# Splitting the PSUM banks of an attention's scores by the engine that empties them, on one Trainium2 core

## The chip, the core and the metric

The program runs on one core of one Trainium2 chip. The metric is the device time of one execution in microseconds, the median over the runs shown. A core has TensorE (matmuls, transposes and the loads of their weights), VectorE, ScalarE, GpSimd, the queues that start transfers, and a PSUM of eight banks of 128 partitions x 512 fp32 values, into which TensorE writes. In the profile the engines are PE (PEld for weight loads), DVE, ACT, POOL and SP.

## The reference

A block on x of 1024 rows and 512 columns, all in fp32, batch 1. Four layers with residuals stand one after the other:

```python
x = x + attn_a(layernorm(x))      # 32 heads of width 16, rotary, causal, full softmax
x = x + ffn(layernorm(x))         # 8 experts of rank 16, top 2, beside a dense base
x = x + attn_b(layernorm(x))      # 32 query heads, 8 key heads of width 128, alibi
x = x + ffn(layernorm(x))
```

The change touches the first attention alone. Cut to what matters:

```python
xq, xk, xv = (x @ w.T).reshape(B, T, 32, 16)       # for wq, wk, wv
xq, xk = rotary_pos_emb(xq), rotary_pos_emb(xk)
scores = einsum('bqhd,bkhd->bhqk', xq, xk) * 16 ** -0.5
probs = softmax(where(causal, scores, -1e30))
out = einsum('bhqk,bkhd->bqhd', probs, xv).reshape(B, T, 512) @ wo.T
```

## The kernel before

The first attention takes about the first 413 us of the span. Heads are padded from 16 to 32 values, so that four heads fill the 128 partitions: there are eight groups of four heads (`NCA` = 8, index c; the head inside a group is j).

The scores are made twice. **Row scores** (`row_scores`, L296; tiles named s) have queries on partitions; VectorE reduces each tile to the negated maximum of every row (`maxima`, L311: a TENSOR_REDUCE at L319 for unmasked pieces, a custom masked reduce at L322 for the others). The maxima are transposed (`with_maxima`, L333, tile tp_m), copied, and put by four small transfers into a spare row of qT, so that **column scores** (`col_scores`, L347; tiles named sT, keys on partitions) come out with the maximum already subtracted. A bf16 matmul of an identity and a mask is added on the diagonal (L372), and ScalarE takes the exponential of each tile (`exponentials`, L374) into p. `product` (L376) multiplies the values by p, in pieces of four matmuls of 32 output columns each.

A score matmul contracts 32 rows, those of one head, so the matmuls of four heads use four row groups of TensorE and can run side by side. Each is made of two fp32 passes.

`step(rc, cc, n)` (L433) does step n (0 to 9) for the row scores of group rc and the column scores of group cc. In the main loop (L477) rc = c + 1 and cc = c, and a step has two halves. A half makes two column tiles and two row tiles, in turn: sT, s, sT, s (`drain` takes one matmul from each generator in turn). The heads are crossed: with rows of heads 0 and 1 go columns of heads 2 and 3, and the other way round. After each half stand VectorE's maxima and ScalarE's exponentials, and then one piece of a product that is three steps old, as long as there is one left (L460, L461). In the seven passes c = 0 to 6 both kinds are made; in the last pass only column scores, and before the main loop the row scores of group 0 are made alone, four tiles at a time (L468 to L474), between the projections.

The projections (`project_a`, L150) take each block of 128 rows through layernorm, a transpose to channels (L206), the projections pj_q, pj_k and pj_v (L176), the rotation by ScalarE and VectorE (L182), and the transposes back into qT and kT (`to_rows`, L192): per block tp_aq and tp_ak, each in two halves. The half with c0 = 0 is copied by VectorE, the other by ScalarE.

Every one of these tiles takes one whole bank. All but the product's accumulator come out of one pool of seven banks, tag "s":

```python
ps_s = ctx.enter_context(tc.tile_pool(name="a_s", bufs=7, space=PSUM))
ps_o = ctx.enter_context(tc.tile_pool(name="a_o", bufs=1, space=PSUM))
```

A pool hands out the bank that is planned to come free first, and TensorE's first matmul into a tile waits until the last reader of the bank's former tile has ended. Each engine takes its instructions in the order of the program that is built; a few of them are placed by the planner and not by the source.

After the last pass `tail` (L996) gathers and projects the first two blocks of the output (tp_ao, pm_ao) around the last normalization (tp_o, L403 to L419), and the feed-forward layer takes over.

Of the kernel before, what the change touches and what calls it, by code (L numbers as in the profile page):

```python
# [9 lines left out]
F32 = mybir.dt.float32  # L10
# [4 lines left out]
PSUM = bass.MemoryType.PSUM  # L15

P = 128
T = 1024
NT = T // P
C = 512  # L20
KC = C // P
QC = 512
# [42 lines left out]
class Block:  # L65
# [58 lines left out]
    def attention_a(self, ctx_pool, wqT, wkT, wvT, rot, midway, tail):  # L124

        nc, tc = self.nc, self.tc

        xnT = ctx_pool.tile([P, NT, KC, P], F32, tag="o", name="xnTa")
        xnTs = [xnT[:, i] for i in range(NT)]
        with ExitStack() as ctx:
            ap = ctx.enter_context(tc.tile_pool(name="a_qkv", bufs=1))
            qT = ap.tile([P, NCA, T], F32, tag="qT", name="qT")
            kT = ap.tile([P, NCA, T], F32, tag="kT", name="kT")
            v_p = ap.tile([P, NT, HA + 1, DA + 1], F32, tag="v_p", name="v_p")  # L140
            nc.gpsimd.memset(v_p[:, :, :HA, DA : DA + 1], 1.0)
            nc.gpsimd.memset(v_p[:, :, HA, :], 0.0)
            ps_s = ctx.enter_context(tc.tile_pool(name="a_s", bufs=7, space=PSUM))
            ps_o = ctx.enter_context(tc.tile_pool(name="a_o", bufs=1, space=PSUM))
            pt = ctx.enter_context(tc.tile_pool(name="a_pt", bufs=5))
            work = ctx.enter_context(tc.tile_pool(name="a_x", bufs=4))
            project_qk, project_v = self.project_a(ap, pt, work, ps_s, xnTs, qT, kT, v_p, wqT, wkT, wvT, rot)
            return self.attend_a(ctx_pool, pt, work, ps_s, ps_o, qT, kT, v_p, project_qk, project_v, midway, tail)

    def project_a(self, ap, pt, work, ps_s, xnTs, qT, kT, v_p, wqT, wkT, wvT, rot):  # L150

        nc = self.nc

        w = {}

        def load(n, src, queue):
            w[n] = pt.tile([P, KC, C], F32, tag="p", name=f"w{n}")
            queue.dma_start(w[n], src.rearrange("(k p) n -> p k n", p=P))

        load("q", wqT, nc.scalar)  # L160
        rt = ap.tile([P, 4, NT], F32, tag="rot", name="rot_sb")
        nc.sync.dma_start(rt, rot)
        load("k", wkT, nc.sync)
        for i in range(2, NT):
            self.load_x(i)
        load("v", wvT, nc.sync)
        for n in range(6):
            self.transpose4(ps_s, [self.ident] * 4, f"i{n}", tag="s")
        rows = {}
        for n, fill in (("q", 0.0), ("k", 1.0)):  # L170
            t = pt.tile([P, 2, HA, PADA], F32, tag="p", name=f"r{n}")
            nc.gpsimd.memset(t[:, :, :, DA : DA + 1], fill)
            nc.gpsimd.memset(t[:, :, :, DA + 1 : PADA], 0.0)
            rows[n] = [t[:, a] for a in range(2)]

        def project(i, n):  # L176
            ps = ps_s.tile([P, C], F32, tag="s", name=f"pj_{n}{i}")
            for kc in range(KC):
                nc.tensor.matmul(ps, lhsT=xnTs[i][:, kc, :], rhs=w[n][:, kc, :], start=(kc == 0), stop=(kc == KC - 1))  # L179
            return ps  # L180

        def rotate(i, n, r, ps):  # L182
            cos, sin = rt[:, r, i : i + 1], rt[:, r + 1, i : i + 1]
            xs = work.tile([P, C], F32, tag="w", name=f"xs_{n}{i}")
            nc.scalar.activation(xs, ps, AF.Copy, scale=sin)
            pv = ps.rearrange("p (h d two) -> p h d two", d=DA // 2, two=2)
            sv = xs.rearrange("p (h d two) -> p h d two", d=DA // 2, two=2)
            dv = rows[n][i % 2][:, :, :DA].rearrange("p h (d two) -> p h d two", two=2)
            nc.vector.scalar_tensor_tensor(dv[:, :, :, 0], pv[:, :, :, 0], cos, sv[:, :, :, 1], ALU.mult, ALU.subtract)
            nc.vector.scalar_tensor_tensor(dv[:, :, :, 1], pv[:, :, :, 1], cos, sv[:, :, :, 0], ALU.mult, ALU.add)  # L190

        def to_rows(i, n, dst):  # L192

            for c0 in range(0, NCA, 4):
                src = [rows[n][i % 2][:, (c0 + c) * 4 : (c0 + c + 1) * 4, :].rearrange("p h d -> p (h d)") for c in range(4)]
                ps = self.transpose4(ps_s, src, f"a{n}{i}_{c0}", tag="s")
                copy = nc.scalar.copy if c0 else nc.vector.tensor_copy
                copy(dst[:, c0 : c0 + 4, i * P : (i + 1) * P], ps)

        pending = []  # L200

        def project_qk():
            def layernorm(i):
                return self.normalized(i, work.tile([P, C], F32, tag="w", name=f"xn_a{i}"), "a", in_order=True)

            def columns(i, xn):  # L206
                self.channels(xn, xnTs[i], ps_s, f"a{i}", tag="s")

            columns(0, layernorm(0))
            for i in range(NT):  # L210
                ps = project(i, "q")
                xn = layernorm(i + 1) if i + 1 < NT else None
                rotate(i, "q", 2, ps)
                if i + 1 < NT:
                    columns(i + 1, xn)
                rotate(i, "k", 0, project(i, "k"))
                while pending:
                    to_rows(*pending.pop(0))
                pending.extend([(i, "q", qT), (i, "k", kT)])
                yield  # L220

        def project_v():
            for i in range(NT):
                ps = project(i, "v")
                while pending:
                    to_rows(*pending.pop(0))
                nc.scalar.copy(v_p[:, i, :HA, :DA], ps.rearrange("p (h d) -> p h d", d=DA))
                yield

        return project_qk(), project_v()  # L230

    def attend_a(self, ctx_pool, pt, work, ps_s, ps_o, qT, kT, v_p, project_qk, project_v, midway, tail):
        nc, tc = self.nc, self.tc
        HC = P // PADA
        with ExitStack() as ctx:
            cp = ctx.enter_context(tc.tile_pool(name="a_c", bufs=1))
            qk = ctx.enter_context(tc.tile_pool(name="a_qk", bufs=2))
            o_sb = []

# [47 lines left out]
            def row_pieces(n):  # L287
                return list(placed(by_rows[n], lambda i, kc: min(QC, (i + 1) * P - kc * QC)))
# [7 lines left out]
            def row_scores(c, n, heads, made):  # L296

                for j in heads:
                    made[j] = ps_s.tile([P, QC], F32, tag="s", name=f"s{c}_{n}_{j}")
                for i, kc, at, end in row_pieces(n):  # L300
                    for j in heads:
                        nc.tensor.matmul(  # L302
                            made[j][:, at:end],
                            lhsT=qT[rows_of(j), c, i * P : (i + 1) * P],
                            rhs=kT[rows_of(j), c, kc * QC : kc * QC + end - at],
                            start=True,
                            stop=True,
                        )
                        yield
# [23 lines left out]
            def with_maxima(c, half):  # L333

                rows = HC * NT // 2
                ps = ps_s.tile([P, QC], F32, tag="s", name=f"tp_m{c}{half}")[:rows, :P]
                nc.tensor.transpose(ps, neg(c, half).rearrange("p h i -> p (h i)"), self.ident)
                t = qk.tile([P, P], F32, tag="negT", name=f"negT{c}_{half}")[:rows, :]
                nc.scalar.copy(t, ps)
                for j in range(HC):  # L340
                    row = j * PADA + DA
                    nc.sync.dma_start(
                        qT[row : row + 1, c, half * QC : (half + 1) * QC].rearrange("o (i t) -> o i t", t=P),
                        t[j * NT // 2 : (j + 1) * NT // 2, :],
                    )

            def col_scores(c, n, heads, made):  # L347

                pieces = col_pieces(n)
                for j in heads:  # L350
                    made[j] = ps_s.tile([P, QC], F32, tag="s", name=f"sT{c}_{n}_{j}")
                for x, (qc, b, at, end) in enumerate(pieces):
                    for j in heads:
                        nc.tensor.matmul(  # L354
# [48 lines left out]
            def normalize(c, qc, oT):  # L403
                if not o_sb:
                    o = ctx_pool.tile([P, NT, C], F32, tag="o", name="o")
                    o_sb.extend(o[:, i] for i in range(NT))
                ps = self.transpose4(ps_s, [oT[:, i * P : (i + 1) * P] for i in range(4)], f"o{c}{qc}", tag="s")
                pv = ps.rearrange("p a (h d) -> p a h d", d=PADA)
                os = qk.tile([P, 4, HC, DA + 1], F32, tag="os", name=f"os{c}_{qc}")
                nc.scalar.copy(os, pv[:, :, :, : DA + 1])  # L410
# [698 lines left out]
```

## Time and profile before

| what | value |
|---|---|
| median of 3 runs | 1683.34 us (1683.14 to 1686.43) |
| the profiled execution: its time | 1683.11 us |
| its span, first to last instruction | 1681.3 us |
| instructions | 32166 |
| granted TensorE clock | 1.000 |
| first attention's main loop, seven passes | 122 to 386 us |

The profile is of one execution. A row of the timeline gives start, length, engine, line, operation, output and inputs, shapes and count, and in brackets how long the engine idled before it and what ended that. Names in it leave out numbers: s stands for every row-score tile, sT for every column-score tile. An engine counts as busy as soon as one of its instructions runs, so four matmuls side by side and one alone look the same in the share of busy time.

### The profile page before, as it was taken

To read this page: it belongs to the slowest core of one execution; us is meant where nothing else is said; L and a number is where in the kernel's file an instruction comes from. 1 tells how busy PE (TensorE), PEld (TensorE's weight loads), DVE (VectorE), ACT (ScalarE), POOL (GpSimd) and SP (SyncE) were. 2 spreads that over 40 slices of the span, in tenths; PEclk is the share of its full clock that TensorE was granted. 3 is DMA by queue.
4 is the path that set the end of the run, shared out by engine and by line. 5 is a ranking of instruction groups with operands and counts; after the bars stand their busy time and mean duration, and the time that the engine had idled before them with its cause. 6 is when DMAs were issued, how large, how long until landed. Compare 5 with 4: busy or idle time off the path is not lost.

```text
span 1681.3 us, 32166 instructions
## 1 busy us (share of the span) xinstructions
PE 1652.6 (98%) x13016; PEld 940.7 (56%) x13016; DVE 1103.0 (66%) x2856; ACT 542.1 (32%) x1217; POOL 347.8 (21%) x508
## 2 busy tenths in 40 slices
PE   9999999999999999999999999999999999999988
PEld 5544444344555667556655665756655665566654
DVE  3556666662653886776677667676677766776773
ACT  2315555555111332233233223223223322322220
POOL 2000000000312332222123212222222321221140
PEclk9999999999999999999999999999999999999999
DMA  5000000001003201100200200110020020000001
GB/s 195 1 1 2 2 2 2 2 2 38 2 24 88 65 2 41 49 26 26 64 26 26 61 30 1 51 38 26 26 64 26 26 71 26 1 27 27 2 1 50
DMA packets 60868, 52.06 MB, mean 31 GB/s; under 512 B 5744, under 2 KB 47472, under 8 KB 60720
## 3 DMA queue, kind: packets, MB, share of 16 engines
q1 hardware_dynamic: 59408, 46.06, 9.2%
q0 software_dynamic: 784, 2.90, 0.4%
q8 instruction: 102, 1.67, 0.4%
q10 hardware_dynamic: 528, 1.05, 0.2%
q14 instruction: 46, 0.38, 0.1%
HBM read 30.98 MB, written 2.10 MB: 20 GB/s over the span
## 4 chain that ended last, share of the span: by engine, by line
PE 87%; DVE 10%; ACT 1%; POOL 1%; issue 1%; DVEq 0%; ACTq 0%; POOLq 0%
PE o L835 13%; PE pq L745 12%; PE s L791 12%; PE wo L642 9%; PE sT L354 7%; PE kv L700 7%; PE oT L389 5%; PE s L302 4%; PE pm_f L599 3%; PE or L835 3%; DVE p L793 3%; DVE nm L797 2%; DVE pT L818 2%; PE pj_v L179 2%; PE pm_ao L993 2%; PE pj_k L179 2%
## 5 line engine op out<-in xcount | busy, mean ns | idle before, releaser
L803 POOL TENSOR_SCALAR p<-p,rs 128x128 f32<-128x128 f32 (+7 forms) x256 | 190.8, 747 | 750.6 <-DVE rs L802 685.7
L800 ACT ACTIVATE p<-p,nm 128x128 f32<-128x128 f32 (+7 forms) x256 | 198.1, 774 | 453.4 <-DVE nm L798 443.0
L793 DVE SCALAR_TENSOR_TENSOR p<-s,rq,rel 128x512 f32<-128x512 f32 (+3 forms) x384 | 227.1, 605 | 119.4 <-PE s L791 118.8
L791 PE MATMUL s<-kT,qT 128*128 128x512 f32 (+3 forms) x768 | 294.8, 492 | 1.8 <-DVE p L793 1.5
L745 PE MATMUL pq<-xnTb,wq 128*128 128x512 f32 x512 | 246.2, 599 | 0.0
L642 PE MATMUL wo<-wo,oT 128*128 128x512 f32 x512 | 241.8, 594 | 3.4 <-DVE x L647 1.9
L791 PEld LDWEIGHTS s<-kT,qT 128*128 128x128 f32 x768 | 141.2, 190 | 165.8 <-issue 126.1
L835 PEld LDWEIGHTS o<-pT,va 32*128 32x128 f32 x5632 | 215.7, 185 | 28.5 <-DVE rs L802 11.8
L835 PE MATMUL o<-pT,va 32*128 32x128 f32 (+7 forms) x5632 | 224.6, 313 | 0.8
L818 DVE STREAM_TRANSPOSE pT<-p 128x640 f32<-128x640 f32 (+4 forms) x256 | 172.1, 673 | 73.1 <-PE o L835 54.7
L374 ACT ACTIVATE p<-sT 128x512 f32<-128x512 f32 (+1 forms) x320 | 157.5, 555 | 113.4 <-PE sT L372 70.9
L797 DVE TENSOR_REDUCE nm<-p 128x1 f32<-128x128 f32 (+7 forms) x256 | 188.2, 736 | 3.6
L302 PE MATMUL s<-kT,qT 32*128 32x512 f32 (+3 forms) x768 | 181.9, 522 | 0.0
L354 PE MATMUL sT<-qT,kT 32*128 32x512 f32 (+3 forms) x768 | 155.7, 521 | 0.0
L642 PEld LDWEIGHTS wo<-wo,oT 128*128 128x128 f32 x512 | 93.8, 190 | 87.5 <-issue 72.4
L745 PEld LDWEIGHTS pq<-xnTb,wq 128*128 128x128 f32 x512 | 92.3, 190 | 87.9 <-issue 80.2
L700 PE MATMUL kv<-wkv,xnTb 128*128 128x256 f32 x512 | 116.7, 382 | 4.4 <-DVE nm L798 4.0
L700 PEld LDWEIGHTS kv<-wkv,xnTb 128*128 128x128 f32 x512 | 95.8, 190 | 26.2 <-DVE nm L798 6.9
L319 DVE TENSOR_REDUCE part<-s 128x1 f32<-128x512 f32 x128 | 80.8, 684 | 40.6 <-PE s L302 36.0
L354 PEld LDWEIGHTS sT<-qT,kT 32*128 32x128 f32 x768 | 60.5, 183 | 62.2 <-issue 24.0
L860 ACT COPY oT<-o 128x1024 f32<-128x1024 f32 (+1 forms) x36 | 33.0, 916 | 181.8 <-PE o L835 176.6
L302 PEld LDWEIGHTS s<-kT,qT 32*128 32x128 f32 x768 | 76.4, 183 | 25.7 <-ACT p L374 10.3
(153 smaller groups left out, 1610.4 us busy)
## 6 DMA issues: line engine op xcount, KB each, us to landing
va<-v SPq DMA_DIRECT2D x256, 64.0 KB
wq<-in_b_WqT_dram SPq DMA_DIRECT2D x8, 1024.0 KB
wo<-in_b_WoT_dram SPq DMA_DIRECT2D x8, 1024.0 KB
x<-in_x_dram SPq DMA_DIRECT2D x8, 256.0 KB
wkv<-in_b_WkT_dram SPq DMA_DIRECT2D x8, 256.0 KB
wkv<-in_b_WvT_dram SPq DMA_DIRECT2D x8, 256.0 KB
out_dram<-x SPq DMA_DIRECT2D x8, 256.0 KB
wq<-in_a_wqT_dram ACTq DMA_DIRECT2D x1, 1024.0 KB
```

The lines of the kernel that those rows point to most:

```text
L302: nc.tensor.matmul(made[j][:, at:end], lhsT=qT[rows_of(j), c, i * P : (i + 1) * P], rhs=kT[rows_of(j), c, kc * QC : kc * QC + end - at], s ...
L354: nc.tensor.matmul(made[j][:, at:end], lhsT=kT[rows_of(j), c, b * P : (b + 1) * P], rhs=qT[rows_of(j), c, (qc + 1) * QC - (end - at) : (qc ...
L642: nc.tensor.matmul(ps, lhsT=oTs[g, h][:, t * P : (t + 1) * P], rhs=wo[:, h, :], start=(h == heads[0]), stop=(h == heads[-1]))
L700: nc.tensor.matmul(ps.rearrange("p a b -> p (a b)"), lhsT=xnT[:, kc, i * P : (i + 1) * P], rhs=wkv[:, kc].rearrange("p a b -> p (a b)"), s ...
L745: nc.tensor.matmul(ps, lhsT=wq[:, kc, hh * DB : (hh + 1) * DB], rhs=xnT[:, kc, cols], start=(kc == 0), stop=(kc == KC - 1))
L791: nc.tensor.matmul(s, lhsT=qT[:, i * P : (i + 1) * P], rhs=kT[:, lo:hi], start=True, stop=True)
L793: nc.vector.scalar_tensor_tensor(p[:, lo:hi], s, rq[:, i : i + 1], rel[:, at + lo : at + hi], ALU.mult, ALU.add)
L797: nc.vector.tensor_reduce(nm, p[:, :w], AX.X, ALU.max, negate=True)
L800: nc.scalar.activation(p[:, :w], p[:, :w], AF.Exp, bias=nm, scale=slope, accum_out=ss)
L803: nc.gpsimd.tensor_scalar(p[:, :w], p[:, :w], rs, 1.0, ALU.mult, ALU.mult)
L818: nc.vector.transpose(PT[:, i : i + (NT - 1) * (m - 1) + 1 : NT - 1, :], p[:, : m * P].rearrange("p (j k) -> p j k", k=P))
L835: nc.tensor.matmul(cols(o[:, a], j), lhsT=vs[g][rows, j * NB + b, :], rhs=moving(j, rows, slice(b * B, (b + 1) * B)), start=(j == js[0] an ...
```

## The change

The pool of seven banks becomes two: `ps_s` with three banks (tag "s") and `ps_c` with four (tag "c"); the pool of the accumulator stays. What VectorE empties goes to `ps_s`: row-score tiles and the first transposes of `to_rows`. What ScalarE empties goes to `ps_c`: column-score tiles, transposes to channels, the other transposes of `to_rows`, tp_m and tp_o; the projections go there too. Where a step makes four row tiles alone, the fourth comes from `ps_c`; where it makes four column tiles alone, the first two come from `ps_s`. The tail takes its tiles from `ps_s`. Nothing that is computed changes.

```diff
-            ps_s = ctx.enter_context(tc.tile_pool(name="a_s", bufs=7, space=PSUM))
+            ps_s = ctx.enter_context(tc.tile_pool(name="a_s", bufs=3, space=PSUM))
+            ps_c = ctx.enter_context(tc.tile_pool(name="a_c", bufs=4, space=PSUM))
             ps_o = ctx.enter_context(tc.tile_pool(name="a_o", bufs=1, space=PSUM))
...
         def project(i, n):
-            ps = ps_s.tile([P, C], F32, tag="s", name=f"pj_{n}{i}")
+            ps = ps_c.tile([P, C], F32, tag="c", name=f"pj_{n}{i}")
...
-                ps = self.transpose4(ps_s, src, f"a{n}{i}_{c0}", tag="s")
+                ps = self.transpose4(*((ps_c, src, f"a{n}{i}_{c0}", "c") if c0 else (ps_s, src, f"a{n}{i}_{c0}", "s")))
                 copy = nc.scalar.copy if c0 else nc.vector.tensor_copy
...
             def columns(i, xn):
-                self.channels(xn, xnTs[i], ps_s, f"a{i}", tag="s")
+                self.channels(xn, xnTs[i], ps_c, f"a{i}", tag="c")
...
                 for j in heads:
-                    made[j] = ps_s.tile([P, QC], F32, tag="s", name=f"s{c}_{n}_{j}")
+                    pool, tag = (ps_c, "c") if len(heads) == HC and j == HC - 1 else (ps_s, "s")
+                    made[j] = pool.tile([P, QC], F32, tag=tag, name=f"s{c}_{n}_{j}")
...
-                ps = ps_s.tile([P, QC], F32, tag="s", name=f"tp_m{c}{half}")[:rows, :P]
+                ps = ps_c.tile([P, QC], F32, tag="c", name=f"tp_m{c}{half}")[:rows, :P]
...
                 for j in heads:
-                    made[j] = ps_s.tile([P, QC], F32, tag="s", name=f"sT{c}_{n}_{j}")
+                    pool, tag = (ps_s, "s") if len(heads) == HC and j < 2 else (ps_c, "c")
+                    made[j] = pool.tile([P, QC], F32, tag=tag, name=f"sT{c}_{n}_{j}")
...
-                ps = self.transpose4(ps_s, [oT[:, i * P : (i + 1) * P] for i in range(4)], f"o{c}{qc}", tag="s")
+                ps = self.transpose4(ps_c, [oT[:, i * P : (i + 1) * P] for i in range(4)], f"o{c}{qc}", tag="c")
```

The rest of the diff hands `ps_c` down to these functions, and gives a pool in SBUF that was named "a_c" the name "a_m".

More of the change, by code (lines that the diff above doesn't have):

```diff
@@ L146, in attention_a, with project_a @@
             work = ctx.enter_context(tc.tile_pool(name="a_x", bufs=4))
-            project_qk, project_v = self.project_a(ap, pt, work, ps_s, xnTs, qT, kT, v_p, wqT, wkT, wvT, rot)
-            return self.attend_a(ctx_pool, pt, work, ps_s, ps_o, qT, kT, v_p, project_qk, project_v, midway, tail)
-    def project_a(self, ap, pt, work, ps_s, xnTs, qT, kT, v_p, wqT, wkT, wvT, rot):
+            project_qk, project_v = self.project_a(ap, pt, work, ps_s, ps_c, xnTs, qT, kT, v_p, wqT, wkT, wvT, rot)
+            return self.attend_a(ctx_pool, pt, work, ps_s, ps_c, ps_o, qT, kT, v_p, project_qk, project_v, midway, tail)
+    def project_a(self, ap, pt, work, ps_s, ps_c, xnTs, qT, kT, v_p, wqT, wkT, wvT, rot):
         nc = self.nc
@@ L230, in project_a, with attend_a @@
         return project_qk(), project_v()
-    def attend_a(self, ctx_pool, pt, work, ps_s, ps_o, qT, kT, v_p, project_qk, project_v, midway, tail):
+    def attend_a(self, ctx_pool, pt, work, ps_s, ps_c, ps_o, qT, kT, v_p, project_qk, project_v, midway, tail):
         nc, tc = self.nc, self.tc
@@ L235, in attend_a @@
         with ExitStack() as ctx:
-            cp = ctx.enter_context(tc.tile_pool(name="a_c", bufs=1))
+            cp = ctx.enter_context(tc.tile_pool(name="a_m", bufs=1))
             qk = ctx.enter_context(tc.tile_pool(name="a_qk", bufs=2))
```

## The prediction

> **What bounds the kernel now.** I read the page first, then the stretch of the first attention by stage, then who waits there, and last the single instructions around those waits.
>
> ```profile
> PE 1652.6 (98%) x13016; PEld 940.7 (56%) x13016; DVE 1103.0 (66%) x2856; ACT 542.1 (32%) x1217; POOL 347.8 (21%) x508
> ```
>
> TensorE is busy for 98% of the span, so time is won or lost only where TensorE is late. By stages (columns: stretch, its length, then busy time and instructions of PE, PEld, DVE, ACT, POOL, then clock and DMA):
>
> ```profile
> 62.00:92.00 30.00, 28.65 (x136) 15.30 (x129) 17.37 (x54) 7.53 (x13) 0.55 (x1) 1.00 0.00 1
> 160.00:197.80 37.80, 37.70 (x358) 15.39 (x358) 25.63 (x83) 21.78 (x47) 2.09 (x8) 1.00 0.01 2
> 386.00:413.00 27.00, 25.64 (x279) 11.73 (x277) 0.61 (x3) 20.89 (x46) 2.09 (x8) 1.00 0.01 2
> ```
>
> The middle row is one pass of the main loop (one c, 37.8 us). There are seven such passes (c = 0 to 6, from 122 to 386 us), then one with column scores alone. VectorE works 25.6 us of a pass and ScalarE 21.8: neither is the bound by its work. But "busy" hides something. In a half step four matmuls on four row groups run side by side; undisturbed they take 1.07 us (171.49 to 172.56 in the timeline). If one of the four must wait for a bank, the other three finish and TensorE still counts as busy. The waits of one pass (engine, line, waited for, us, times, longest):
>
> ```profile
> PEld s L302 <- ACT p L374: 1.5, 3, 0.6
> PEld s L302 <- DVE neg L322: 0.3, 1, 0.3
> ```
>
> So it is a row-score tile whose weight load is held up. The timeline at step n = 4 and at step n = 5 of this pass:
>
> ```profile
> 172.65 1.08 ACT L374 ACTIVATE p<-sT 128x512 f32<-128x512 f32 x2 [1.09 <-PE s L302]
> 172.69 1.29 DVE L319 TENSOR_REDUCE part<-s 128x1 f32<-128x512 f32 x2 [0.94 <-PE s L302]
> 172.92 0.69 PE L302 MATMUL s<-kT,qT 32*128 32x512 f32 x1
> 173.30 0.69 PE L302 MATMUL s<-kT,qT 32*128 32x512 f32 x1
> ...
> 176.08 1.57 ACT L374 ACTIVATE p<-sT 128x512 f32<-128x512 f32 x3 [0.38 <-PE s L302]
> 176.12 1.89 DVE L319 TENSOR_REDUCE part<-s 128x1 f32<-128x512 f32 x3 [0.71 <-PE s L302]
> 176.72 0.29 PEld L302 LDWEIGHTS s<-kT,qT 32*128 32x128 f32 x2 [0.64 <-ACT p L374]
> ```
>
> The first row tile starts at 172.92 with the others, the second only at 173.30: that is 0.05 us after ScalarE's first exponential of the half before has ended (172.65 + 0.60 = 173.25). The same at 176.72 (176.08 + 0.60 + 0.05). It is the first column tile of the half before whose bank the late row tile takes over.
>
> **The change part by part.** No instruction is added or removed, and the order on each engine is the same but for two swaps (s_2_2 and s_2_3 at 83 us, and tp_o before pm_ao at 413 us). What changes is who held each bank before, and so whom TensorE waits for.
>
> *Main loop.* Row tiles now rotate over three banks, two per half. The tile three places back is: for the first row tile of a half the second of two halves ago, long read; for the second row tile the first row tile of the half just before. So in every half the second row tile waits for VectorE's first read of the half before. Column tiles rotate over four, two per half, so they take banks two halves old; I cost them at nothing (a pass gives ScalarE 37.8 us for 21.8 of work). With seven shared banks the kernel before, as it is built, already has the VectorE dependency in steps 0 to 3 and 7 (second half) to 9; those keep their waits (0.3 at 161.72, 0.6 at 165.80, 0.4 at 169.66, 0.14 in each of steps 8 and 9). It has the ScalarE dependency in the first halves of steps 4, 5, 6 and 7, and these four move. (Some second halves of steps 1 to 6 move too, but a product stands in front of them and their banks are free by then.) What each release costs:
>
> ```profile
> L374 ACT ACTIVATE p<-sT 128x512 f32<-128x512 f32 x224 | 120.1, 597 | 88.5 <-PE sT L372 50.1 <-PE s L302 30.9 <-PE sT L354 5.8
> L319 DVE TENSOR_REDUCE part<-s 128x1 f32<-128x512 f32 x112 | 70.8, 684 | 33.1 <-PE s L302 28.6 <-PE sT L354 3.6
> ```
>
> VectorE takes 684 ns where ScalarE takes 597 (mean of one), and starts 0.04 to 0.05 us later (172.69 against 172.65, 176.12 against 176.08, 180.67 against 180.62, 184.10 against 184.05). So its release comes 0.087 + 0.045 = 0.13 us later. Step 4: 172.69 + 0.68 + 0.05 = 173.42 in place of 173.30; step 5: 176.85 for 176.72; step 6: 181.40 for 181.27; step 7: 184.83 for 184.70. VectorE had been idle before each of these reads (0.94, 0.71, 1.47 and 0.94 us), so nothing queued in front of it makes it worse. The late tile is the last of its half, and behind it on TensorE stands a product or a transpose [...], so the delay goes straight into the path: 4 x 0.13 = 0.53 us a pass, 7 passes, +3.7 us. Lower bound 0.09 each if the start gap vanishes (2.4), upper 0.16 (4.5).
>
> [...] 25.6 us of VectorE in 37.8, idle before the reads, and in the second halves a product of 0.4 to 1 us stands between. The nearest to deciding is step 4, second half: its first-half tile ends near 173.90, is read until about 174.80, and is wanted at 174.92. I take 3.7.
>
> *Projections and the first row scores (up to 122 us).* At each of the steps n = 0 to 3 of the lone row scores, three of the four tiles need the three row banks, and these also carry the first transposes of q and k (tp_aq, tp_ak with c0 = 0), which VectorE copies. In the changed kernel as it is built the third row tile takes the bank of tp_ak, issued just before it; in the kernel before it has an older bank. The timeline at n = 2:
>
> ```profile
> 82.19 1.04 PE L99 MATMUL tp_ak<-ident,rk 128*128 128x128 f32 x8
> 82.95 0.48 DVE L190 SCALAR_TENSOR_TENSOR rk<-pj_k,rot_sb,xs_k 128x256 f32<-128x256 f32 x1
> 83.16 0.71 PE L302 MATMUL s<-kT,qT 32*128 32x256 f32 x8
> 83.34 0.68 DVE L198 COPY kT<-tp_ak 128x512 f32<-128x512 f32 x1
> 83.80 3.70 PE L179 MATMUL pj_v<-wv,xnTa 128*128 128x512 f32 x8
> ```
>
> The copy ends at 84.02, so the third tile starts at 84.07 instead of 83.17: +0.90, and pj_v behind it too. The same copy stands at 73.46 for n = 1 (74.19 for 73.28, +0.91), at 88.85 for n = 3 (89.59 for 89.20, +0.39) and at 61.59 for n = 0 (+0.90). The first of these is covered: behind it TensorE idles anyway, waiting for the layernorm that VectorE makes after the maxima, and VectorE itself is not late.
>
> ```profile
> 67.53 0.63 PE L99 MATMUL tp_a<-ident,xn_a 128*128 128x128 f32 x4 [1.35 <-DVE xn_a L115]
> ```
>
> 1.35 us of idle swallow the 0.90; without that cover it would cost 0.9. The other three have no idle behind them (the next rows of TensorE follow without a gap): +2.2 us. Later steps have 4.7 us per step and older banks: nothing. Bounds 1.3 (one more hidden) and 3.1.
>
> *Last pass and tail.* In the last pass column tiles use both pools, two each; ScalarE (20.9 of 27 us) frees them in the same order as before: 0, give or take 0.3. In the tail tp_o moves ahead of pm_ao0 into an idle gap of 0.35 us, and frees POOL's four multiplies (419.03, 1.04 us) from standing in front of the rsqrt of the next layernorm, behind which TensorE idles 0.87 at 422.09. I take -0.5, between 0 and -0.9.
>
> *Sum.* +3.7 + 2.2 - 0.5 = +5.4 us. Everything behind 455 us is unchanged and starts later as a whole. The profiled execution took 1683.1 us (span 1681.3 and 1.8 around it), 0.2 under the median of the runs, 1683.34. So 1683.2 + 5.4 = 1688.6 us.
>
> **The rivals.**
>
> Faster: the separation takes the late row tile away. In steps 4 to 7 a pass loses 0.36 + 0.83 + 0.83 + 0.14 = 2.2 us to it (from the start it would have had beside its three fellows). If the row bank were free before the half starts, seven passes would give 15.4 us back, and with the projections at +2.2 and the tail at -0.5 the time would be about 1669.5. It decides from the point where VectorE has read the first row tile before the next half begins, 172.92 in step 4. For it: column tiles no longer wait for VectorE at all. Against it: the read ends at 173.37, and 0.94 us of idle before it show that it cannot start earlier.
>
> No change: the main loop costs only its lower bound of 2.4, the projection waits are swallowed like the first one down to 0.5, and the tail gives its 0.9: +2.0, 1685.2. For it: TensorE has 1.35 us of slack in that stretch (28.65 of 30). Against: that slack is the one gap already used.
>
> Backlog: VectorE is pushed so that second halves wait as well, four more places of 0.13 in each pass: +3.7 on top, 1692.3. For it the thin margin in step 4 (174.80 + 0.05 against 174.92); against it that the half itself then starts 0.13 later as well.
>
> That the pools end up sharing banks after all is ruled out: they are three different pools, of 3, 4 and 1 banks.
>
> **How the numbers follow.** A difference of 0.2% (3.4 us) is about what a measurement of this kernel can tell. Forecast case 0.76 (1686.7 to 1691; its bounds together give +2.8 to +7.9, and what falls under +3.4 counts with no change), backlog 0.07, no change 0.13, faster 0.04. Slower by over 0.2% is the first two, 0.83. The range must leave no more than 2 in 10 outside: I go from 1685.5 (part of the no-change case) to 1691.0 (projections at 3.1 and releases at 0.16).
>
> **What would show it.** Right: the third and fourth row tile at n = 1 to 3 of the lone steps start after DVE L198's copy; in a pass the wait "PEld s <- ACT p" is gone and "PEld s <- DVE part" stands in its place; a pass takes 38.3 us; sT starts near 124 us and pm_ao near 419. Wrong: a pass of 37.8 or less (the release gap is not 0.13 or not on the path), or projections that end where they ended before.

## The result and the profile after

| | kernel before | changed kernel |
|---|---|---|
| median, us | 1684.05 (8 runs, 1683.05 to 1686.43) | 1688.55 (8 runs, 1688.12 to 1689.99) |
| ratio to before, 95% interval | | 1.0028 (1.0017 to 1.0039) |
| span of the profiled execution, us | 1681.3 | 1688.1 |
| granted TensorE clock over the span | 1.000 | 0.999 |

The change makes the kernel slower by 4.5 us by the medians; the interval of the ratio allows 2.9 to 6.6. Executions whose granted clock was 1.000 took 1688.12 to 1688.35 us in the changed kernel (4 of the 8) and 1682.91 to 1683.43 in the kernel before (11 of the 49 that the first experiments are set against), about 5 us apart by their medians. The two profiled spans lie 6.8 us apart; the last section says where the 1.5 us above the steady difference come from. The page's first part looks as before, PE at 98% again:

```profile
PE 1661.2 (98%) x13016; PEld 943.2 (56%) x13016; DVE 1104.8 (65%) x2856; ACT 543.2 (32%) x1217; POOL 347.2 (21%) x508
```

The same three stretches of the changed kernel (projections, one pass of the main loop, last pass; stretch, length, then busy time and instructions of PE, PEld, DVE, ACT, POOL, then clock and DMA):

```profile
62.00:92.00 30.00, 29.42 (x130) 15.58 (x128) 15.79 (x52) 7.44 (x12) 0.55 (x1) 1.00 0.00 1
162.30:200.60 38.30, 38.19 (x358) 15.55 (x354) 25.75 (x83) 21.82 (x47) 2.09 (x8) 1.00 0.01 2
391.80:418.90 27.10, 26.16 (x281) 11.81 (x277) 0.64 (x3) 20.99 (x46) 2.09 (x8) 1.00 0.01 2
```

VectorE's and ScalarE's work in a pass is what it was (25.75 and 21.82 us), but the pass is longer. Measured from the transpose tp_m in one pass to the same one in the next it takes 38.36 us (165.59 to 203.95) where before took 37.80 (163.01 to 200.81). This is how every pass below is measured. Who the row tiles wait for in that pass (engine, tile, line, waited for, us in total, times, longest):

```profile
PEld s L305 <- DVE part L322: 2.0, 4, 0.8
...
PEld s L305 <- DVE neg L325: 0.3, 1, 0.3
```

The wait for ScalarE's p is gone, and four waits for VectorE's part stand in its place. The timeline of the changed kernel at step n = 4, and then at n = 5:

```profile
175.23 1.08 ACT L378 ACTIVATE p<-sT 128x512 f32<-128x512 f32 x2 [1.15 <-PE s L305]
175.27 1.29 DVE L322 TENSOR_REDUCE part<-s 128x1 f32<-128x512 f32 x2 [0.94 <-PE s L305]
...
175.50 0.69 PE L305 MATMUL s<-kT,qT 32*128 32x512 f32 x1
...
176.01 0.29 PEld L305 LDWEIGHTS s<-kT,qT 32*128 32x128 f32 x2 [0.21 <-DVE part L322]
176.02 0.69 PE L305 MATMUL s<-kT,qT 32*128 32x512 f32 x1
```

```profile
178.79 1.58 ACT L378 ACTIVATE p<-sT 128x512 f32<-128x512 f32 x3 [0.43 <-PE s L305]
178.84 1.29 DVE L322 TENSOR_REDUCE part<-s 128x1 f32<-128x512 f32 x2 [0.85 <-PE s L305]
...
179.58 0.29 PEld L305 LDWEIGHTS s<-kT,qT 32*128 32x128 f32 x2 [0.78 <-DVE part L322]
```

At n = 4 the first row tile starts at 175.50 and the second at 176.02: 0.52 us apart, where before they were 0.38 apart. 175.27 + 0.69 + 0.05 = 176.01 is the end of VectorE's first read and the same 0.05 us that stood between ScalarE's end and TensorE before. Means of one read, over the main loop by operation and shape (count, then busy us and mean ns, then idle before):

```profile
L378 ACT ACTIVATE p<-sT 128x512 f32<-128x512 f32 x224 | 120.1, 597 | 90.3 <-PE sT L376 52.1 <-PE s L305 32.6 <-PE sT L358 5.1
...
L322 DVE TENSOR_REDUCE part<-s 128x1 f32<-128x512 f32 x112 | 72.2, 686 | 34.5 <-PE s L305 29.7 <-PE sT L358 3.6
```

In the projections, step n = 2 of the changed kernel:

```profile
82.87 1.04 PE L99 MATMUL tp_ak<-ident,rk 128*128 128x128 f32 x8
83.83 0.71 PE L305 MATMUL s<-kT,qT 32*128 32x256 f32 x6
...
84.03 0.68 DVE L200 COPY kT<-tp_ak 128x512 f32<-128x512 f32 x1
84.76 0.69 PE L305 MATMUL s<-kT,qT 32*128 32x256 f32 x2 [0.22 <-DVE kT L200]
...
85.39 1.13 PE L181 MATMUL pj_v<-wv,xnTa 128*128 128x512 f32 x2
```

Before, all eight matmuls of the four row tiles (two records for each tile) stood in one row at 83.16, and pj_v followed at 83.80. Now six start together, two wait for the copy of tp_ak to end (84.03 + 0.68 = 84.71), and TensorE does nothing else until then.

### The profile page after: what moved, and what is told of

Same layout as the page of the kernel before. It is cut to its first block, busy times and chain, and to the rows that moved or that the text cites. A ratio compares the mean times of both kernels' runs of the same rounds, so it can differ in the third digit from the quotient of the medians.

```text
span 1688.1 us, 32102 instructions
## 1 busy us (share of the span) xinstructions
PE 1661.2 (98%) x13016; PEld 943.2 (56%) x13016; DVE 1104.8 (65%) x2856; ACT 543.2 (32%) x1217; POOL 347.2 (21%) x508
## 4 chain that ended last, share of the span: by engine, by line
PE 86%; DVE 10%; POOL 1%; ACT 1%; issue 1%; DVEq 0%; ACTq 0%; POOLq 0%
PE o L839 13%; PE pq L749 12%; PE s L795 12%; PE wo L646 9%; PE sT L358 7%; PE kv L704 7%; PE oT L393 5%; PE s L305 4%; PE pm_f L603 3%; PE or L839 3%; DVE p L797 3%; DVE nm L801 2%; DVE pT L822 2%; PE pj_v L181 2%; PE pm_ao L997 2%; PE pj_k L181 2%
## 5 line engine op out<-in xcount | busy, mean ns | idle before, releaser
L305 PE MATMUL s<-kT,qT 32*128 32x512 f32 (+3 forms) x768 | 188.6, 523 | 0.2 <-DVE kT L200 0.2
L322 DVE TENSOR_REDUCE part<-s 128x1 f32<-128x512 f32 x128 | 82.1, 686 | 42.4 <-PE s L305 37.6
```

The source lines that it names most:

```text
L305: nc.tensor.matmul(made[j][:, at:end], lhsT=qT[rows_of(j), c, i * P : (i + 1) * P], rhs=kT[rows_of(j), c, kc * QC : kc * QC + end - at], s ...
```

## The experiments

Medians below are set against runs of the kernel before in the same series (1684.82, 1684.75 and 1684.47 us, in this order for the first four kernels, the next three, and the last). The question for the first four: are the two terms of the sum, bank release in the main loop and bank release in the projections, what they were taken for?

**lone2: the lone row-score steps take two tiles from each pool.** An edit to the changed kernel:

```diff
-                    pool, tag = (ps_c, "c") if len(heads) == HC and j == HC - 1 else (ps_s, "s")
+                    pool, tag = (ps_c, "c") if len(heads) == HC and j >= HC - 2 else (ps_s, "s")
```

> The changed kernel, but where a step makes four row tiles alone, two of them (not one) come from the pool of four banks; the three row banks then carry two row tiles beside the transposes that VectorE copies. If the 2.0 us lost before 122 us come from the third row tile waiting for VectorE's copy of tp_ak, they go: column scores start at 121.8 as in the kernel before, not at 123.7, and the main loop keeps its 38.3 us a pass; the whole about 1686.5 us, 2 less than the changed kernel. If they come instead from the projections, which now share four banks with ScalarE's transposes, two more tiles in that pool make it worse: later than 123.7, over 1689.

Measured: 1687.05 us, ratio to before 1.0016 (1.0009 to 1.0023). The column scores start at 121.64 us where the changed kernel starts them at 123.67 and before at 121.68. The same n = 2 in lone2:

```profile
83.11 0.71 PE L305 MATMUL s<-kT,qT 32*128 32x256 f32 x8
83.21 0.59 ACT L200 COPY kT<-tp_ak 128x512 f32<-128x512 f32 x1 [0.29 <-PE tp_ak L99]
83.30 0.68 DVE L200 COPY kT<-tp_ak 128x512 f32<-128x512 f32 x1
83.75 0.30 PEld L181 LDWEIGHTS pj_v<-wv,xnTa 128*128 128x128 f32 x2 [0.33 <-DVE rk L192]
```

All eight row-score matmuls start together again and pj_v follows without waiting for the copy. So the 2 us come from the third row tile alone, and not from the projections' own move to ps_c, which lone2 keeps. The main loop keeps its loss: the pass is 38.36 us, and its waits from 124 to 390 us are those of the changed kernel (14.0 us in 28 waits there):

```profile
PEld s L305 <- DVE part L322: 13.9, 28, 0.8
```

**half_after and half_before: VectorE reads half of each row tile.** The same edit in the changed kernel (L322) and in the kernel before (L319):

```diff
-                            nc.vector.tensor_reduce(parts[c, i][:, j : j + 1], s, AX.X, ALU.max, negate=True)
+                            nc.vector.tensor_reduce(parts[c, i][:, j : j + 1], s[:, : w // 2], AX.X, ALU.max, negate=True)
```

> The changed kernel, but the unmasked row maxima (TENSOR_REDUCE) are taken over the first half of each piece only, so part of the maxima is left out. That read falls from 0.68 to about 0.42 us and the row bank comes free 0.27 us earlier. If the second row tile of the first halves of steps 4 to 7 waits for exactly this read, each of these four places in a pass gets 0.27 us back: 4 x 0.27 x 7 = 7.5 us less than the changed kernel, about 1681, below the kernel before; a pass of 37.2 us. If the loss of the changed kernel lies in the split of the pool as such (fewer banks to choose from, or column tiles), the reads of VectorE are hidden and the time stays at 1688 to 1689.

> The kernel before with the same shorter read of the unmasked row maxima (half of each piece is left out of them). By the theory that there the four late row tiles wait for ScalarE's exponential, a shorter VectorE read gives nothing: within 0.5 us of the kernel before, a pass of 37.8 us. If VectorE's reads set the pace in both kernels, it falls by several us too (up to 7.5).

Measured: half_after 1682.64 us, ratio 0.9986 (0.9979 to 0.9992), pass 37.28; half_before 1683.63 us, ratio 0.9995 (0.9987 to 1.0004), pass 37.79. The read in half_after:

```profile
L322 DVE TENSOR_REDUCE part<-s 128x1 f32<-128x256 f32 x112 | 43.8, 422 | 51.7 <-PE s L305 41.9 <-PE sT L358 8.3
```

It is 264 ns shorter than the full read (686 - 422). With four places a pass that is 4 x 0.264 = 1.06 us, and the pass fell by 1.08 (38.36 to 37.28). The row tiles' waits from 124 to 390 us, in half_after and then in half_before:

```profile
PEld s L305 <- DVE part L322: 7.1, 14, 0.5
```

```profile
PEld s L302 <- ACT p L374: 10.3, 20, 0.6
```

The 28 waits of the changed kernel became 14, two a pass: the two long ones of a pass fell from 0.78 to 0.51 us, and the two short ones are too short to be listed. In the kernel before, the same saving on VectorE does nothing: its row tiles wait for ScalarE, in the same 20 waits of 10.3 us in all, and its pass stays at 37.8. That is the strongest evidence that the change handed the wait from ScalarE's read to VectorE's. The whole gain is a little smaller than seven passes make it (7.6 us): behind the tail, at tp_f, half_after is 6.8 us ahead of the changed kernel (420.64 for 427.43), and by the medians 5.9. The 0.7 between them is lost in the first 8 us, which the edit doesn't touch: the first transposes start 0.21 us apart there, up to 7.3 us, and 0.11 apart in the changed kernel, and from the first projection on (8.41 for 7.68) the offset stays at 0.74.

**rows4: four banks for the row side and three for the column side.** An edit to the changed kernel:

```diff
-            ps_s = ctx.enter_context(tc.tile_pool(name="a_s", bufs=3, space=PSUM))
-            ps_c = ctx.enter_context(tc.tile_pool(name="a_c", bufs=4, space=PSUM))
+            ps_s = ctx.enter_context(tc.tile_pool(name="a_s", bufs=4, space=PSUM))
+            ps_c = ctx.enter_context(tc.tile_pool(name="a_c", bufs=3, space=PSUM))
```

> The changed kernel with the sizes turned round: four banks for row tiles, three for column tiles. Row tiles then take banks two halves old and never wait; the second column tile of a half takes the bank of the first column tile of the half before, that is it waits for ScalarE's exponential, which comes after the mask matmul where there is one, and the transposes tp_m and tp_o compete for the same three banks. If only the engine that releases mattered (0.60 us of ScalarE for 0.68 of VectorE), a pass would come back to 37.8 us or less and the time to 1684 to 1686. If what the three-bank side carries matters more, the column side is the worse one to squeeze, since it carries the masks and the two transposes: a pass of about 39 us, 1692 to 1694.

Measured: 1693.96 us, ratio 1.0054 (1.0042 to 1.0067): slower still. The column scores start at 121.72, so the fourth row bank removes the projections' loss, but the pass is 38.65. Waits of the row and column tiles from 124 to 390 us, in the changed kernel and then in rows4:

```profile
PEld sT L358 <- ACT p L378: 22.8, 48, 0.8
PEld s L305 <- DVE part L322: 14.0, 28, 0.8
```

```profile
PEld sT L358 <- ACT p L378: 34.7, 77, 0.8
...
PEld s L305 <- DVE part L322: 1.6, 7, 0.2
```

The row tiles' wait nearly goes, and the column tiles' wait grows by about as much. ScalarE's read is the shorter one (597 ns for 686 in the changed kernel), so if the releasing engine alone decided, rows4 would have been near the kernel before. It isn't. Compared with the kernel before, matmul by matmul, a pass of rows4 loses about 0.6 us from step 1 to the start of step 3, where tp_m and tp_o take banks of the column pool and the column tiles have a mask matmul ahead of their exponentials. It loses nothing in step 5, where tp_o and tp_m stand as well but no mask (the offset is 2.45 us before and 2.47 behind), and the rest comes from step 8 on. Which of the two, the transposes or the masks, makes the loss was not separated. The last pass adds to it: from its tp_m to pm_ao the changed kernel takes 25.08 us (394.43 to 419.51) and rows4 26.97 (395.95 to 422.92). What exactly is late in rows4's last pass was not followed up.

**due5_before and cut_before: cover in front of the waiting half.** The latest of the late row tiles, in the first halves of steps 5 and 6, start 0.83 us after their three fellows (a row of waits shows 0.6 of it, since it counts from the end of the weight load before). There two halves of scores follow each other on TensorE with nothing between. These two edits of the kernel before put needed work there. In due5_before the transposes tp_o and tp_m of step 5 go ahead of its first half:

```diff
                 both = rc is not None and cc is not None
+                while due and both and n in (5,):
+                    due.pop(0)()
                 for half in range(2 if both else 1):
```

In cut_before the product of n = 2 comes in two pieces of 128 columns. A product stands two steps behind its exponentials, not three, so this one is worked off in step 4, and its second piece now ends that step:

```diff
-                    cut = w // 2 if w == QC and not first else w
+                    cut = w // 2 if n == 2 or (w == QC and not first) else w
...
-                                stop=last,
+                                stop=last and x1 == w,
```

> The kernel before, with the two transposes that follow the first half of step 5 (tp_o and tp_m) moved ahead of that half, so that they stand between two halves that otherwise follow each other without any other work. Nothing is left out. If the 0.83 us that the second row tile is late there are a plain wait for ScalarE's first exponential, the transposes (0.4 us and 0.1, [...]) cover most of it and the late start shrinks to 0.1 to 0.3 us; [...] a pass falls from 37.8 to 37.3 to 37.6 us and the whole by 1.5 to 3.5 us, to 1681.5 to 1683. If the transposes have their own wait (the copy of oT, or the bank), nothing is gained: 1684 to 1686.

> The kernel before, with the one product piece of n = 2 (256 columns) cut into two of 128, so that the second half of step 4 also gets a product behind it. Nothing is left out. The piece of 0.57 us becomes two of about 0.36; the second covers part of the 0.83 us wait at step 5. Theory of a plain wait: a pass falls by 0.2 to 0.4 us, the whole by 1.5 to 3 us, to 1682 to 1683.5. [...]

Measured: due5_before 1683.08 us, ratio 0.999 (0.9981 to 0.9998), pass 37.58; cut_before 1683.23 us, ratio 0.9991 (0.9984 to 0.9997), pass 37.57. Both gain 0.22 to 0.23 us a pass. Both show this line from 124 to 390 us:

```profile
PEld s L302 <- ACT p L374: 4.5, 7, 0.6
```

Seven waits are left of twenty: one a pass, at step 6. In cut_before the late tile of step 5 starts 0.32 us after its fellows (176.17 for 175.85) instead of 0.83. Of the half microsecond 0.15 goes to the second piece (two of 0.36 us from start to start for one of 0.57) and about as much to the half in front of it, which takes 1.12 us now that it isn't followed directly by the next, and 0.96 before. What is left is the 0.2 us gained.

**due5_lone2: the first cover in the kernel lone2.** The edit is that of due5_before, made to lone2.

> The changed kernel with two of the four lone row tiles from the pool of four (as in lone2) and with tp_o and tp_m ahead of the first half of step 5. By the theory three of the four moved places in a pass stay (0.14 each) and the one at step 5 is covered: a pass of 37.9 to 38.1 us and 1684.5 to 1686, still not below the kernel before with the same move. If splitting the pool helps once the back-to-back halves are apart, it falls below due5_before.

Measured: 1685.49 us, ratio to before 1.0005 (0.9998 to 1.0012), pass 38.01 where lone2 has 38.36. From 124 to 390 us:

```profile
PEld s L305 <- DVE part L322: 6.9, 14, 0.8
```

With separate pools the same cover is worth 0.35 us a pass, more than in the kernel before, because there is more wait to cover (the tile of step 5 is 0.97 us late there, not 0.83). It still does not reach the kernel before.

**due6cut: both places covered.** cut_before takes care of step 5, so tp_o and tp_m can be held back for step 6. An edit to cut_before:

```diff
-                due = list(later)
-                later.clear()
+                due = []
+                if n != 5 or rc is None or cc is None:
+                    due = list(later)
+                    later.clear()
...
+                    while due and both and n == 6:
+                        due.pop(0)()
                     gens = []
```

> The kernel before with both covers: the product of n = 2 in two pieces (one stands between the two halves of step 5), and tp_o and tp_m held back from step 5 to the front of step 6's first half, the second place where two halves follow each other with nothing between and a row tile waits 0.83 us. If the wait is plain waiting that any needed work on TensorE covers, the two gains add: the cut alone gave 0.23 us a pass against before, moving tp_o and tp_m over a wait of the same size another 0.2 or so, pass near 37.35, seven passes 1.5 us below the cut alone, median near 1681.7, and 'PEld s L302 <- ACT p L374' nearly gone from a pass. The rival: each place taken from one wait opens another (step 5 loses the 0.7 us that tp_o and tp_m stood in front of its product, and its second half then waits for VectorE's or ScalarE's reads), so the pass stays near 37.57 and the median near 1683.2.

Measured: 1681.73 us, ratio to before 0.9983 (0.9976 to 0.999), pass 37.37. The gains add: 37.80 before, 37.57 with one place covered, 37.37 with two. Of the row tiles' waits for reads this is all that is left from 124 to 390 us:

```profile
PEld s L302 <- DVE neg L322: 1.5, 5, 0.3
```

This version beats both kernels, with the seven shared banks of the kernel before: 2.7 us below it and, by medians of different series, 6.8 below the changed one.

## Why the prediction was right

The forecast was 1688.6 and the median is 1688.55. That they agree so closely is luck: the sum starts from 1683.2, which is 0.85 below the later median of the kernel before, and its +5.4 is 0.9 above the 4.5 between the medians. The terms are not luck. The forecast's sum is made against one profiled execution, so it is compared with the traces, matmul by matmul in TensorE's order (start in the changed kernel less start before):

| step of the sum | predicted | in the traces |
|---|---|---|
| projections, to the first column scores | +2.2 | +2.0 (121.68 to 123.67) |
| main loop, seven passes | +3.7 | +3.8 (from +1.99 to +5.81) |
| tail, to the first transpose behind it (tp_f) | -0.5 | -0.47 (from +5.81 to +5.34) |
| sum | +5.4 | +5.3; 4.5 by the medians |

*Main loop.* The four places a pass are where they were said to be, and each adds 0.14 where 0.13 was predicted. Steps 4 to 7 of the shown pass start their late tile at 176.02, 179.58, 184.28 and 187.84; the offset against before goes from 2.58 to 2.72, 2.86, 3.00 and 3.14. In step 5 the transposes behind the late tile follow at its end, and so take the delay on: its two matmuls run to 179.58 + 1.12 = 180.70, and tp_o starts at 180.64. Seven passes of this are 28 x 0.14 = 3.9. At one place the offset falls back by 0.27 (277 us, at the start of the fifth pass): there the kernel before lost 0.27 that the changed one did not. Why was not settled. At the start of the last pass 0.1 is added. half_after and half_before show that it is VectorE's read that these places wait for now, and that it was not before.

*The other halves.* A pass has 20 halves, and the traces have four places in it at which the change adds anything. With 25.75 us of work in 38.36 VectorE, which empties the row tiles, is not the bottleneck; what costs is one particular tile whose bank was read last just before.

*Projections.* The size is nearly right for the reason given. At n = 1, 2 and 3 the offset grows by 0.94, 0.91 and 0.40 (predicted 0.91, 0.90, 0.39). At n = 0 the third tile is late too (its last matmul starts 0.74 later, at 62.69 for 61.95), and the idle time behind it swallows that, as the sum had it:

```profile
67.27 0.66 PE L99 MATMUL tp_a<-ident,xn_a 128*128 128x128 f32 x4 [0.35 <-DVE xn_a L115]
```

1.35 us of idle became 0.35. tp_a even starts 0.26 us earlier than before, which makes 2.0 of the 2.2; 0.14 to 0.24 of that lead is there from the first microseconds on (19.27 for 19.41) and has nothing to do with the change. lone2 shows that the third tile's bank alone is the cause.

*Tail.* tp_o starts at 419.00, ahead of pm_ao at 419.51, and tp_f comes at 427.43 for 422.09. The size is right, but of the two reasons given only the first shows: 0.44 is gained by the second pm_ao (from +5.87 to +5.43), as tp_o no longer stands between the two and the idle 0.35 ahead of the first is used. The idle time in front of tp_f, which the freeing of POOL was to shorten, fell from 0.87 to 0.78 only, and it ends on VectorE's addition to x in both kernels. This term was not tested by itself.

*The rivals.* That the late row tile would vanish did not happen: its bank is read by VectorE until 175.96, and it was wanted at 175.50. That the gap would be hidden is refuted by lone2, which wins back the 2 us. That the second halves would wait as well is not seen: all jumps of the offset in a pass are at first halves, four in number. A rival that the prediction does not list, since it costs the column tiles at nothing, is that these pay for their smaller pool. Their waits of over 0.15 us from 124 to 390 us come to 28.7 us in the changed kernel (22.8 for ScalarE's p, shown above, and 5.9 for its copy negT). In the kernel before these four rows, with 32.4 us, stand in their place, so they don't wait longer than before:

```profile
PEld sT L354 <- ACT p L374: 15.1, 29, 0.8
...
PEld sT L354 <- DVE rsa L412: 5.9, 7, 0.8
PEld sT L354 <- DVE part L319: 5.8, 14, 0.4
PEld sT L354 <- DVE neg L322: 5.6, 14, 0.4
```

## What to carry to other kernels

When pools are split, ask of each tile which earlier tile's bank it takes over, on which engine that tile's last read runs, and when that read ends against the moment the new tile is wanted; the busy shares of the engines (here 67% and 57% of a pass) say nothing about it. Splitting seven banks into three and four cost time here in two ways. In the main loop the four late tiles of a pass take over a bank that is as recent as before (the half step just ahead), but one that the slower of two reads gives free. In the lone row scores the third tile takes over a more recent bank. Where two groups that need the same banks follow each other with nothing between, moving work that has to be done anyway into that place was worth 0.2 us at each place in a pass, while none of the three groupings of the banks that were tried gained anything.

## What the hardware showed that was not expected

From the tail to 1642 us the changed kernel stands 5.2 to 5.4 us behind before, and then it loses more in work that the change doesn't touch. The stretch from one transpose to the next product, in the changed kernel and then in the kernel before at the same place in the program (columns as above, the last but two the granted clock):

```profile
1648.00:1652.00 4.00, 4.00 (x12) 2.32 (x12) 0.69 (x1) 0.58 (x1) 0.00 (x0) 0.59 0.02 4
```

```profile
1643.00:1647.00 4.00, 4.00 (x20) 2.56 (x19) 1.38 (x2) 0.86 (x2) 0.00 (x0) 1.00 0.06 22
```

And the rows around it in the changed kernel:

```profile
1647.36 0.99 PE L99 MATMUL tp_g_f<-ident,g_f 128*128 128x128 f32 x4 [1.81 <-DVE g_f L588]
1648.15 1.06 PE L99 MATMUL tp_f<-ident,xn_f 128*128 128x128 f32 x4
1649.00 1.91 PE L603 MATMUL pm_f<-w_base,xnT_f 128*128 128x512 f32 x2
```

TensorE's granted clock is one half for 3.41 us:

```profile
1647.89:1651.30 3.41, 3.41 (x9) 2.11 (x9) 0.69 (x1) 0.58 (x1) 0.00 (x0) 0.50 0.02 5
```

In the 4 us shown first there are 12 matmuls where before had 20, the four transposes tp_f take 1.06 us instead of 0.60, two products 1.91 instead of 1.02. That is about 1.5 us more (pr_f, behind these, starts at 1651.87 for 1645.05, 6.82 later, and tp_f at 1648.15 for 1642.89, 5.26 later), and with it the two profiled spans lie 6.8 apart and the medians 4.5. Why here and not in the kernel before is not shown. These are the 3.41 us ahead of the drop, and then the same stretch in the kernel before, 5.15 us earlier as tp_g_f is (1642.21 for 1647.36):

```profile
1644.48:1647.89 3.41, 1.60 (x7) 0.62 (x5) 3.04 (x17) 0.00 (x0) 0.00 (x0) 1.00 0.00 0
```

```profile
1639.33:1642.74 3.41, 1.59 (x7) 0.62 (x5) 3.03 (x17) 0.00 (x0) 0.00 (x0) 1.00 0.00 0
```

TensorE is busy for 47% of both, 1.60 and 1.59 us, and the idle time ahead of tp_g_f is 1.81 and 1.82 us. Behind the one the clock is one half, behind the other it stays at 1.00, so the work of this stretch does not tell the two apart.

The profiled executions differ in their clock as well. Over the span it is 0.998 in due5_lone2, 0.999 in the changed kernel, lone2, half_after, half_before, rows4 and due6cut, and 1.000 in the kernel before, due5_before and cut_before. Of the changed kernel's 8 runs four have 1.000 and four 0.999, and these four took 1688.76 to 1689.99 us. So a single profiled span can carry 1.5 us that is not the change's, medians mix executions with and without it, and the offset ahead of such a stretch is the better figure.
